# Two small transposes moved from TensorE to VectorE, in blocks of 32, in a fused window-attention and expert kernel

## The chip, the core and the metric

The kernel runs on one core of a Trainium2 chip. The core has a matmul engine (TensorE, PE in the profile), a vector engine (VectorE, DVE), a scalar engine (ScalarE, ACT), GpSimd (POOL), and SyncE (SP), whose queue issues most of the transfers here. They run side by side and wait for each other by semaphores. The metric is device time in microseconds; 4548.22 us is the median of three runs of the kernel before (4543.13 to 4551.57).

## The reference, cut to what matters

The input x is (2, 128, 256, 256) in float32: 131,072 pixels ("tokens") of 128 channels. One layer adds two things to it.

```
x = x + conv(ln_c(x))        # window attention, 8x8 windows, keys from 12x12, 4 heads of 32
t = tokens(x)
t = t + ffn(ln_t(t))         # 8 experts, the best two of each token

def ffn(x):
    p = softmax(x @ router_w + router_b)
    top_p, top_i = top_k(p, 2);  top_p = top_p / sum(top_p)
    y = einsum('bnd,edc->bnec', x, expert_w) + expert_b
    return sum over the two of top_p * y[top_i]
```

`ln_c` and `ln_t` normalise each token over its 128 channels. The mask of the attention leaves only keys whose row and column offsets have the right parity, so queries split into four interleaved "planes".

The change touches how, for each token, the mean, the mean square and the router's eight raw logits become gates (eight weights, of which two aren't zero) and two scale or shift values, and how these reach the places where they are used.

## The kernel before

**Tiling.** The image is cut into strips of eight rows; a strip has four planes of 512 queries. One turn of the main loop (`for n in range(n_planes + 7)`) handles one plane's attention, prepares the next plane's projections, and runs one expert "row" of 512 tokens (two image rows) of the strip before. There are 256 planes, and some turns at the end without attention. Channels lie on the 128 partitions. Tokens lie along the free dimension, 512 to a row, in NT = 4 groups of 128.

**Order.** The loop stands under a manual schedule: instructions stand on each engine in the order in which the code calls them. Functions are generators; each `next(...)` emits one piece of one. Each engine works its own queue in order. At the start of a turn PE's instructions are aligned (`addr_align(BLOCK, ...)`, L786).

**The row's statistics and gates.** `norms` (L531) squares the source (L541, ScalarE) and multiplies source and square by the narrow matrix `rw` (L547, PE). This puts, for each group t of 128 tokens, the logits (8), mean and mean square into the 32 partitions 32t to 32t+31 of the PSUM tile `plt`, with tokens along the columns. ScalarE copies it to SBUF (`lT`, L555) and PE transposes it whole into `plg` (L558), so that tokens lie on partitions: 128 partitions x (4 groups x 32 values). `rstd` (L227 to L234, with two exponents on ScalarE, L231 and L232) gives the reciprocal deviation. `norms` can serve two rows at once: f, the row for the experts, and c, a row for the attention's own normalisation.

`route` (L582 to L615, VectorE) makes logits, ranks, and gates, into `g`: 128 partitions x 40 columns, of which 32 are gates (expert by group), 4 the shift (`sd`, L590) and 4 the scale of row c (L567).

`spread` (L622 to L630) transposes g on PE into `pg`, copies it by ScalarE into `gT` (L624), writes gT to a DRAM tile `gd` (L626), and reads row c's scale back, broadcast to all partitions, as `rb` (L630). The experts read their gates back in the same way: `fetch` reads one expert's 512 gates into all 128 partitions (`gb`, L654), `fetch_means` the shift (`sb`, L659). All these reads stand in SyncE's queue.

**The experts.** VectorE multiplies six of the eight (`xe` <- `xs`, `gb`, L670) and GpSimd two, after `behind(6)` (L674) has held GpSimd until VectorE's sixth is done. PE multiplies with the expert's weights and adds up in `acc` (L679); VectorE adds acc to x (L685).

**PSUM.** `mm_tile` hands out tiles from a ring of three (tag mm). A plane takes nine: pvv, pu, pk, pq, pg, plt, pvv, plg, po. A new tile waits until the one three before it has been read.

**Where things stand in a turn.** The part that the change moves is `spread`; it stands after all of the next plane's projections to pq:

```
next(ahead, None)                 # pvv
nxt.fetch(7, nc.scalar)
next(ahead, None)                 # pu, and its block transpose uT on VectorE (L385)
states[n + 1]["shift"]()          # uT -> auT -> au: the position bias's rows (L348, L353)
next(ahead, None); next(ahead, None)   # pk; pq
if gated: gd, rb1 = spread(...)   # pg
for e in (4, 6, 7, 5): ex.product(e)
```

The functions that the diff touches, with the profile's line numbers:

Of the kernel before, what the change touches and what calls it, by code (L numbers as in the profile page):

```python
# [1 line left out]

# [8 lines left out]
F32 = mybir.dt.float32  # L11
AF = mybir.ActivationFunctionType
ALU = mybir.AluOpType
# [3 lines left out]
P = 128  # L17
HEADS, DH = 4, 32
E = 8
# [31 lines left out]
def kernel(  # L51
# [16 lines left out]
    nc = tc.nc  # L68
# [450 lines left out]
    def out_project(n, state):  # L519
# [8 lines left out]
        nc.vector.tensor_add(xv, po.rearrange("p (m a s) -> p m a s", a=PR, s=4), xv)  # L528
        yield

    def norms(f, c, nm):  # L531

        g = small.tile([P, (E + 2) * NT], F32, tag="g", name=f"g{nm}")
        srcs = []
        for j, src in ((0, f and rows_of(*f)), (2, c and ln1_src(*c))):
            if src is None:
                continue
            sq = work.tile([P, CH], F32, tag=f"sq{j}", name=f"sq{j}{nm}", bufs=1)  # L540
            nc.scalar.activation(sq, src, AF.Square)  # L541
            srcs += [(j, src), (j + 1, sq)]
        yield
        plt = mm_tile(f"plt{nm}")
        for j, src in srcs:
            for t in range(NT):
                nc.tensor.matmul(  # L547
                    plt[32 * t : 32 * t + 32, :P],
                    lhsT=rw[:, j],
                    rhs=src[:, t * P : (t + 1) * P],  # L550
                    start=(j == srcs[0][0]),
                    stop=(j == srcs[-1][0]),
                )
        lT = work.tile([P, P], F32, tag="lT", name=f"lT{nm}")
        nc.scalar.copy(lT, plt[:, :P])  # L555
        yield
        plg = mm_tile(f"plg{nm}")
        nc.tensor.transpose(plg[:, :P], lT, ident)  # L558
        p4 = plg[:, :P].rearrange("p (t e) -> p t e", e=32)
        k0, k1 = (0 if f else 1), (2 if c else 1)  # L560
        r, u = rstd(p4, k0, k1, nm)
        rs = None
        if f:
            rs = small.tile([P, NT], F32, tag="rs", name=f"rs{nm}")
            nc.vector.scalar_tensor_tensor(rs, u[:, 0], 3.0, r[:, 0], ALU.add, ALU.mult)
        if c:
            nc.vector.scalar_tensor_tensor(  # L567
                g[:, (E + 1) * NT :], u[:, 1 - k0], 3.0, r[:, 1 - k0], ALU.add, ALU.mult
            )
        yield g, rs, p4  # L570

# [3 lines left out]
    def route(i, k, g, rs, p4):  # L575


        nm = f"{i}_{k}"
        rs = rs.unsqueeze(2)
        lg = small.tile([P, NT, E], F32, tag="lg", name=f"lg{nm}")  # L580
        by_e = [P, NT, E]
        nc.vector.tensor_tensor(lg, p4[:, :, 0:E], rs.broadcast_to(by_e), ALU.mult)  # L582
        nc.vector.tensor_tensor(lg, lg, rb.unsqueeze(1).broadcast_to(by_e), ALU.add)
        mx = small.tile([P, NT, 1], F32, tag="mx2", name=f"mx2{nm}")
        nc.vector.tensor_reduce(mx, lg, AX.X, ALU.max)
        nc.vector.tensor_tensor(lg, lg, mx.broadcast_to(by_e), ALU.subtract)
        nc.scalar.activation(lg, lg, AF.Exp)
        sd = small.tile([P, NT, 1], F32, tag="sd", name=f"sd{nm}")
        nc.vector.reciprocal(sd, rs)
        nc.vector.tensor_tensor(  # L590
            g[:, E * NT : (E + 1) * NT].unsqueeze(2), sd, p4[:, :, E : E + 1], ALU.subtract
        )
        yield

        cmp = small.tile([P, NT, E, E], F32, tag="cmp", name=f"cmp{nm}")
        nc.vector.tensor_tensor(
            cmp,
            lg.unsqueeze(2).broadcast_to([P, NT, E, E]),
            lg.unsqueeze(3).broadcast_to([P, NT, E, E]),
            ALU.subtract,  # L600
        )
        nc.vector.tensor_tensor(
            cmp, cmp, ties.unsqueeze(1).broadcast_to([P, NT, E, E]), ALU.is_ge
        )
        rank = small.tile([P, NT, E], F32, tag="rank", name=f"rank{nm}")
        nc.vector.tensor_reduce(rank, cmp, AX.X, ALU.add)
        yield
        gate = small.tile([P, NT, E], F32, tag="gate", name=f"gate{nm}")
        nc.vector.scalar_tensor_tensor(gate, rank, 1.5, lg, ALU.is_lt, ALU.mult)
        sm = small.tile([P, NT, 1], F32, tag="sm2", name=f"sm2{nm}")  # L610
        nc.vector.tensor_reduce(sm, gate, AX.X, ALU.add)
        nc.vector.reciprocal(sm, sm)
        nc.vector.tensor_tensor(sm, sm, rs, ALU.mult)
        g1 = g[:, 0 : NT * E].rearrange("p (e t) -> p t e", t=NT)
        nc.vector.tensor_tensor(g1, gate, sm.broadcast_to(by_e), ALU.mult)  # L615
        yield

    def spread(f, c, g, nm):

        lo, hi = (0 if f else (E + 1) * NT), ((E + 2) * NT if c else (E + 1) * NT)  # L620
        pg = mm_tile(f"pg{nm}")
        nc.tensor.transpose(pg[: hi - lo, :P], g[:, lo:hi], ident)  # L622
        gT = small.tile([(E + 2) * NT, P], F32, tag="gT", name=f"gT{nm}")
        nc.scalar.copy(gT[: hi - lo], pg[: hi - lo, :P])  # L624
        gd = dram.tile([(E + 2) * NT, P], F32, tag="gd", name=f"gd{nm}")
        nc.sync.dma_start(gd[lo:hi], gT[: hi - lo])  # L626
        rb = None
        if c:
            rb = gates.tile([P, NT * P], F32, tag="rb", name=f"rb{nm}", bufs=2)
            nc.sync.dma_start(rb, to_all(gd, E + 1))  # L630
        return gd, rb
# [139 lines left out]
    with tc.manual_schedule(engines={ET.PE, ET.DVE, ET.Activation, ET.Pool, ET.SP}):  # L771
        for n in range(n_planes + 7):
            i, pl = divmod(n, 4)
            score, attn, outp, ahead, norm, rout = none, none, none, none, none, none
            if n < n_planes:
                score = scores(n, states[n])
                attn = attend(n, states[n])
                outp = out_project(n, states[n])
            if n + 1 < n_planes:
                states[n + 1] = {}  # L780
                ahead = project(n + 1, states[n + 1])

            if 6 <= n < n_planes:
                nc.tensor.addr_align(BLOCK, offset=BLOCK - FIRST_LIMIT)  # L786


            next(score, None)
            new, row = NoExperts(), None  # L790
            if gated and gated[0]:
                rout = route(*gated[0], *gated[2])
            next(rout, None)
            nxt.fetch(5, nc.scalar)
            for _ in rout:
                pass
            next(score, None)
            next(ahead, None)
            nxt.fetch(7, nc.scalar)
            next(ahead, None)  # L800
            if n + 1 < n_planes:
                states[n + 1]["shift"]()
            next(ahead, None)
            next(ahead, None)
            if gated:
                f, c, made = gated
                gd, rb1 = spread(f, c, made[0], f"_{n}")
                row = (*c, rb1) if c else None
                new = Experts(*f, gd) if f else new
            for e in (4, 6, 7, 5):  # L810
                ex.product(e)


            f = (i - 1, pl) if 0 < i <= len(strips) else None
            c = row_at(n)
            if f or c:
                norm = norms(f, c, f"_{n}")
            next(norm, None)
            next(attn, None)
            nxt.means()  # L820
            new.fetch_means()
            for e in (0, 1, 2, 3):
                nxt.times(e, dve)
            new.fetch(0, dve)
            for e in (4, 6):
                nxt.times(e, dve)
            new.fetch(1, dve)
            ex.end()
            new.fetch(2, dve)
            next(attn, None)  # L830
            next(attn, None)


            ex = nxt
            next(norm, None)
            load_x((n + 9) // 4, (n + 9) % 4, paced=True)
            new.fetch(3, dve)
            while to_store:
                store(*to_store.pop())
            next(ahead, None)  # L840
            ex.product(0)
            made = next(norm, None)
            ex.product(1)
            ex.product(2)
            new.fetch(4, nc.scalar)
            nxt.behind(6)
            nxt.times(5, pool)
            if row:
                ln1(*row, pool)
            if pl == 3 and i + 2 < len(strips):  # L850
                halo(i + 2)
            nxt.times(7, pool)
            if n + 2 < n_planes:
                columns(n + 2)
            next(outp, None)
            ex.product(3)
            next(outp, None)
            new.fetch(6, dve)
            gated, nxt = (f, c, made) if made else None, new
            states.pop(n, None)  # L860
# [58 lines left out]
```

The softmax here doesn't subtract the row's maximum and nothing guards it: scores larger than these inputs give would overflow.

## Time and profile before

| what | value |
|---|---|
| time, median of three | 4548.22 us |
| profiled execution | 4547.9 us, mean granted TensorE clock 0.997 |
| the transpose plg, PE (L558) | 260 times, mean 273 ns |
| the copy lT, ScalarE (L555) | 260 times, mean 266 ns |
| the transpose pg, PE (L622) | 245 times with 40 columns of g, mean 270 ns |
| the copy gT, ScalarE (L624) | 245 times with 40 rows, mean 259 ns |
| the write gd (L626) | 245 times with 20.0 KB |
| block transposes of 128x512 on VectorE | L385 and L505 717 ns (from PSUM), L510 711 ns (from SBUF) |
| bytes moved | 824.84 MB, 181 GB/s, 457,786 packets |

How to read it: a row of the groups gives line, engine, operation, tiles (out<-in), shape, count, busy time and mean duration, and then the idle time of the engine just before these instructions and who ended it. Matmuls are pipelined, so their durations overlap; what one takes out of PE's stream is read from the chain of work, where each piece is listed from its predecessor's end. In a timeline, a line gives start, length, engine, line and operation; a bracket gives how long the engine stood idle before it and who released it.

### The profile page before, as it was taken

Reading aid. Unit: us, or ns where it says so; the run is one execution under the profiler, and the core shown is the slowest. Engines: PE = TensorE matmul, PEld = TensorE weight load, DVE = VectorE, ACT = ScalarE, POOL = GpSimd, SP = SyncE. Lnnn points to the kernel's source line nnn. Section 1 sums busy time; section 2 is a strip of 40 time slices with the busy share of each in tenths; the row PEclk is TensorE's granted clock in tenths of the full one; section 3 lists DMA queues with packets and bytes.
Section 4 is the critical chain, followed back from the end, with each engine's and each line's share of the span. In section 5 each row is a group of like instructions: output and inputs, shape, how many; then the busy total and the mean of one; then the engine's idle time right before and its main releaser. Section 6 shows DMA issues by size and latency. Waiting matters only on the chain.

```text
span 4547.9 us, 224166 instructions
## 1 busy us (share of the span) xinstructions
PE 4490.6 (99%) x96841; PEld 2708.2 (60%) x96841; DVE 3826.1 (84%) x11330; ACT 1582.6 (35%) x4542; POOL 1321.7 (29%) x1812
## 2 busy tenths in 40 slices
PE   7999999999999999999999999999999999999997
PEld 5665666565666666666666666666666656656653
DVE  5888888888888888888888888888888888888886
ACT  3333333333333333333333333333333333333331
POOL 1232323232323223232323232323232323232221
PEclk9999999999999999999999999999999999999999
DMA  2565666566556666665656665656666656666655
GB/s 76 176 191 180 190 179 191 181 190 180 189 180 189 183 186 184 186 185 183 188 181 186 183 188 181 190 180 190 180 190 180 191 179 190 182 187 181 188 163 181
DMA packets 457786, 824.84 MB, mean 181 GB/s; under 512 B 52480, under 2 KB 64356, under 8 KB 456804
## 3 DMA queue, kind: packets, MB, share of 16 engines
q1 hardware_dynamic: 456074, 810.21, 59.0%
q8 instruction: 769, 12.60, 1.1%
q14 instruction: 213, 1.74, 0.1%
q10 hardware_dynamic: 730, 0.29, 0.0%
HBM read 737.95 MB, written 72.34 MB: 178 GB/s over the span
## 4 chain that ended last, share of the span: by engine, by line
PE 97%; DVE 1%; issue 1%; DMA 0%; ACT 0%; POOL 0%; SPq 0%; ACTq 0%; DVEq 0%; POOLq 0%
PE acc L679 38%; PE pvv L368 12%; PE att L464 7%; PE att L495 6%; PE plt L547 6%; PE pu L383 5%; PE po L523 5%; PE pk L395 5%; PE pq L417 5%; PE att L447 3%; PE att L485 3%; PE pg L622 1%; PE plg L558 1%; DMA gb<-gd 0%; DVE xe L670 0%
## 5 line engine op out<-in xcount | busy, mean ns | idle before, releaser
L679 PE MATMUL acc<-xe,ew 128*128 128x512 f32 x4096 | 1921.7, 595 | 6.5 <-DVE xt L685 2.6
L679 PEld LDWEIGHTS acc<-xe,ew 128*128 128x128 f32 x4096 | 720.8, 191 | 788.1 <-issue 780.3
L670 DVE TENSOR_TENSOR xe<-xs,gb 128x512 f32<-128x512 f32 x1536 | 950.5, 686 | 10.9 <-DMA gb<-gd 2.2
L674 POOL COPY last<-xe 128x1 f32<-128x1 f32 x256 | 48.3, 189 | 3110.8 <-DVE gb L653 3103.7
L670 POOL TENSOR_TENSOR xe<-xs,gb 128x512 f32<-128x512 f32 x512 | 652.3, 1275 | 5.7 <-PE att L495 2.7
L368 PE MATMUL pvv<-wt,xcol 128*128 128x128 f32 x4096 | 595.1, 288 | 4.2 <-POOL xcol L330 3.1
L368 PEld LDWEIGHTS pvv<-wt,xcol 128*128 128x128 f32 x4096 | 497.2, 191 | 66.6 <-issue 51.9
L555 ACT COPY lT<-plt 128x128 f32<-128x128 f32 x260 | 69.3, 266 | 1141.3 <-PE plt L547 1141.3
L271 POOL TENSOR_TENSOR xn<-xt,rb 128x512 f32<-128x512 f32 x249 | 375.9, 1510 | 79.9 <-DMA rb<-gd 68.1
L464 PE MATMUL att<-qs,kcol 32*64 32x32 f32 x32768 | 391.7, 226 | 2.4 <-issue 2.4
L464 PEld LDWEIGHTS att<-qs,kcol 32*64 32x64 f32 x32768 | 390.3, 130 | 2.6 <-issue 2.6
L375 ACT COPY vv<-pvv 128x512 f32<-128x512 f32 x512 | 300.3, 586 | 207.4 <-PE pvv L368 191.4
L495 PEld LDWEIGHTS att<-pT,vv 64*32 64x32 f32 x32768 | 347.8, 105 | 36.7
L472 ACT ACTIVATE pT<-att 128x1024 f32<-128x1024 f32 x256 | 262.1, 1024 | 253.7 <-PE att L464 250.3
L495 PE MATMUL att<-pT,vv 64*32 64x32 f32 x32768 | 342.5, 200 | 0.0
L385 DVE STREAM_TRANSPOSE uT<-pu 128x512 f32<-128x512 f32 x256 | 183.5, 717 | 150.2 <-PE pu L383 150.2
L541 ACT ACTIVATE sq<-xt 128x512 f32<-128x512 f32 x505 | 292.1, 628 | 0.0
L353 DVE STREAM_TRANSPOSE au<-auT 128x512 f32<-128x512 f32 x256 | 269.2, 1051 | 9.0
L406 ACT COPY kcol<-pk 128x560 f32<-128x560 f32 (+2 forms) x344 | 174.3, 507 | 268.5 <-PE pk L395 265.7
L523 PE MATMUL po<-o,wt 128*128 128x512 f32 x512 | 261.8, 593 | 4.1 <-DVE r__0_619 L227 1.0
L383 PE MATMUL pu<-xn,wrel 128*128 128x512 f32 x512 | 263.6, 596 | 0.0
L417 PE MATMUL pq<-xn,wt 128*128 128x512 f32 x512 | 262.2, 593 | 0.5 <-issue 0.2
(2700 smaller groups left out, 5579.8 us busy)
## 6 DMA issues: line engine op xcount, KB each, us to landing
gb<-gd SPq DMA_DIRECT2D x2048, 256.0 KB
xt<-in_x_dram SPq DMA_DIRECT2D x256, 256.0 KB
sb<-gd SPq DMA_DIRECT2D x256, 256.0 KB
out_dram<-xt SPq DMA_DIRECT2D x256, 256.0 KB
rb<-gd SPq DMA_DIRECT2D x249, 256.0 KB
gd<-gT SPq DMA_DIRECT2D x245, 20.0 KB
ew<-in_L_ffn_expert_w_dram SPq DMA_DIRECT2D x1, 512.0 KB
eb<-in_L_ffn_expert_b_dram SPq DMA_DIRECT2D x1, 512.0 KB
```

The costliest lines, as they stand in the source:

```text
L271: eng.tensor_tensor(xn[i % 2][:, :, :, k, 1 : PC + 1], ln1_src(i, k).rearrange("p (y j x) -> p y x j", y=2, x=2), rb.rearrange("p (y j x) ...
L368: nc.tensor.matmul(pv[:, t * P : (t + 1) * P], lhsT=xl[:, t0 + t].rearrange("p a k -> p (a k)"), rhs=wv, start=True, stop=True,)
L375: nc.scalar.copy(vv[:, t0 : t0 + 4, :].rearrange("p t c -> p (t c)"), pv)
L383: nc.tensor.matmul(pu, lhsT=wrel, rhs=inner, start=True, stop=True)
L417: nc.tensor.matmul(pq, lhsT=wq, rhs=inner, start=True, stop=True)
L464: nc.tensor.matmul(sc[rows, h, 32 * t : 32 * t + 32], lhsT=kk[hp, half * HP + t, :], rhs=qs[hp, m0 : m0 + 2].rearrange("p m a s -> p (m a ...
L495: nc.tensor.matmul(av[hp, half, 32 * t : 32 * t + 32], lhsT=vv[rows, t, hp], rhs=pT[rows, h, 32 * t : 32 * t + 32], start=True, stop=True,)
L523: nc.tensor.matmul(po, lhsT=wo, rhs=state["o"].rearrange("p f z -> p (f z)"), start=True, stop=True)
L541: nc.scalar.activation(sq, src, AF.Square)
L547: nc.tensor.matmul(plt[32 * t : 32 * t + 32, :P], lhsT=rw[:, j], rhs=src[:, t * P : (t + 1) * P], start=(j == srcs[0][0]), stop=(j == srcs ...
L670: eng.tensor_tensor(self.xe[e], self.xs, self.gb.pop(e), ALU.mult)
L679: nc.tensor.matmul(self.acc, lhsT=ew[:, e, :], rhs=self.xe.pop(e), start=(e == 0), stop=not self.xe)
```

## The change

Both full transposes and both copies go. `norms` transposes `plt` on VectorE in 32x32 blocks straight into `plg`, also in PSUM. As tokens were on columns in four blocks of 32, the result has token i of block b of group t on partition 32t+i and its values in columns 32b onward, and no longer one group to 32 columns. Arithmetic on g and plg doesn't mind. `g` becomes a fixed tile of 2 blocks of 32 columns (32 gates; and sd, row c's scale and zeros), three of them in turn, cleared once at the start by GpSimd. `spread` turns its blocks on VectorE into `gT`, and two writes of 32 columns each put them into `gd`, which now has 64 rows: first the half with shift and scale, then the gates. The address pattern of the write brings tokens back into order, in runs of 32 values (128 bytes). And `spread` moves up: it stands after the first piece of the next projection (pvv) and `fetch(7)`, ahead of pu and the position bias's rows. PE thus loses two instructions a plane, the PSUM ring one tile of nine.

```diff
+    gboth = [ctile([P, 2, NT, E], f"g{i}") for i in range(3)]
+    g_turn = itertools.count()
+    for g in gboth:
+        nc.gpsimd.memset(g, 0.0)
...
-        g = small.tile([P, (E + 2) * NT], F32, tag="g", name=f"g{nm}")
+        g = gboth[next(g_turn) % len(gboth)]
...
-        lT = work.tile([P, P], F32, tag="lT", name=f"lT{nm}")
-        nc.scalar.copy(lT, plt[:, :P])
         yield
         plg = mm_tile(f"plg{nm}")
-        nc.tensor.transpose(plg[:, :P], lT, ident)
+        nc.vector.transpose(plg[:, :P], plt[:, :P])
...
-                g[:, (E + 1) * NT :], u[:, 1 - k0], 3.0, r[:, 1 - k0], ALU.add, ALU.mult
+                g[:, 1, :, 1], u[:, 1 - k0], 3.0, r[:, 1 - k0], ALU.add, ALU.mult
...
-            g[:, E * NT : (E + 1) * NT].unsqueeze(2), sd, p4[:, :, E : E + 1], ALU.subtract
+            g[:, 1, :, 0:1], sd, p4[:, :, E : E + 1], ALU.subtract
...
-        g1 = g[:, 0 : NT * E].rearrange("p (e t) -> p t e", t=NT)
-        nc.vector.tensor_tensor(g1, gate, sm.broadcast_to(by_e), ALU.mult)
+        nc.vector.tensor_tensor(g[:, 0], gate, sm.broadcast_to(by_e), ALU.mult)
...
     def spread(f, c, g, nm):
-        lo, hi = (0 if f else (E + 1) * NT), ((E + 2) * NT if c else (E + 1) * NT)
-        pg = mm_tile(f"pg{nm}")
-        nc.tensor.transpose(pg[: hi - lo, :P], g[:, lo:hi], ident)
-        gT = small.tile([(E + 2) * NT, P], F32, tag="gT", name=f"gT{nm}")
-        nc.scalar.copy(gT[: hi - lo], pg[: hi - lo, :P])
-        gd = dram.tile([(E + 2) * NT, P], F32, tag="gd", name=f"gd{nm}")
-        nc.sync.dma_start(gd[lo:hi], gT[: hi - lo])
+        gT = small.tile([P, 2, 32], F32, tag="gT", name=f"gT{nm}")
+        nc.vector.transpose(
+            gT.rearrange("p k i -> p (k i)"), g.rearrange("p k b j -> p (k b j)")
+        )
+        gd = dram.tile([2 * E * NT, P], F32, tag="gd", name=f"gd{nm}")
+        to = gd.rearrange("(k j t) (b i) -> k (t b) j i", k=2, j=E, i=32)
+        for k in (1, 0):
+            if k or f:
+                nc.sync.dma_start(to[k], gT[:, k])
...
             nxt.fetch(7, nc.scalar)
+            if gated:
+                f, c, made = gated
+                gd, rb1 = spread(f, c, made[0], f"_{n}")
+                row = (*c, rb1) if c else None
+                new = Experts(*f, gd) if f else new
             next(ahead, None)
...
             next(ahead, None)
             next(ahead, None)
-            if gated:
-                f, c, made = gated
-                gd, rb1 = spread(f, c, made[0], f"_{n}")
-                row = (*c, rb1) if c else None
-                new = Experts(*f, gd) if f else new
             for e in (4, 6, 7, 5):
                 ex.product(e)
```

More of the change, by code (lines that the diff above doesn't have):

```diff
@@ L1 @@
+import itertools
 from contextlib import ExitStack
```

## The prediction

> **What bounds the kernel now.** I read the busy shares first, then the chain of work that ended last, then that chain over one plane, then the other engines over the same plane.
>
> ```profile
> PE 4490.6 (99%) x96841; PEld 2708.2 (60%) x96841; DVE 3826.1 (84%) x11330; ACT 1582.6 (35%) x4542; POOL 1321.7 (29%) x1812
> ...
> PE 97%; DVE 1%; issue 1%; DMA 0%; ACT 0%; POOL 0%; SPq 0%; ACTq 0%; DVEq 0%; POOLq 0%
> ```
>
> PE holds 97% of the chain, so a microsecond taken out of PE's stream in the loop should come off the end, and work on another engine costs nothing until it makes PE wait. The chain over one plane shows what the two transposes to be removed take there (start, length, piece):
>
> ```profile
> 2000.43 0.86 PE pq L417 x2
> 2001.29 0.11 PE pg L622
> 2001.40 3.44 PE acc L679 x8
> ...
> 2008.66 0.86 PE acc L679 x2
> 2009.52 0.11 PE plg L558
> 2009.63 1.72 PE acc L679 x4
> ```
>
> pg begins the moment pq ends and acc begins 0.11 us later; the same at plg. The mean of 270 ns in the table of groups is latency, not what PE gives up: its stream advances by 0.11. The plane's period is 2023.95 - 2006.56 = 17.39 us (the same piece, plt, one plane later in a longer answer of this view). Now VectorE over the same plane, since it takes over the work:
>
> ```profile
> 2009.10 0.06 DVE L653 MEMSET gb<- 128x1 f32 x1
> 2009.67 0.17 DVE L227 COPY r__114_37583<-plg 128x8 f32<-128x8 f32 x1 [0.51 <-PE plg L558]
> 2009.87 0.50 DVE L228 TENSOR_TENSOR u__114_37582<-r__114_37583 128x8 f32<-128x8 f32 x1
> ...
> 2011.89 0.16 DVE L567 SCALAR_TENSOR_TENSOR g<-u__114_37582,r__114_37583 128x4 f32<-128x4 f32 x1
> 2012.24 0.69 DVE L528 TENSOR_TENSOR xt<-po,xt 128x512 f32<-128x512 f32 x1 [0.20 <-PE po L523]
> ...
> 2016.24 0.22 DVE L615 TENSOR_TENSOR g<-gate,sm 128x32 f32<-128x32 f32 x1
> 2017.00 0.72 DVE L385 STREAM_TRANSPOSE uT<-pu 128x512 f32<-128x512 f32 x1 [0.54 <-PE pu L383]
> ```
>
> VectorE waits for PE three times a plane: 0.51 for plg, 0.20 for po, 0.54 for pu. So it is not the bound, but only about 1.25 us a plane from being it. GpSimd's line in the same window explains L228:
>
> ```profile
> 2009.08 1.27 POOL L670 TENSOR_TENSOR xe<-xs,gb 128x512 f32<-128x512 f32 x1
> ```
>
> L228 multiplies a tile of 8 columns by itself and lasts 0.50 instead of the 0.17 of its neighbours. It ends at 2010.37, GpSimd's product at 2010.35.
>
> **What the Trainium skill says.** "SBUF — State Buffer", section "Who interferes with whom": a VectorE instruction with two SBUF inputs and a GpSimd instruction that reads SBUF exclude each other, and whichever issues second waits for the first to finish; one with at most one SBUF input doesn't contend outside the two-port modes. The trace agrees: L228 (two SBUF inputs) ends with GpSimd's product, L227 (input in PSUM) runs beside it at 0.17. So the statistics can't get past L228 before GpSimd's xe(7) is done, however early they start, and the new transpose of plt (one input, in PSUM) may run beside GpSimd. "VectorE: DVE Perf Modes", section "The three transpose paths": VectorE turns independent 32x32 blocks only. That is why the layout of g and of the writes changes. "DMA: Bandwidth & Descriptors", section "Specifications": below 512 B a transfer loses line rate to a read-modify-write. The new writes go in runs of 128 B; no run here shows that yet, so I bound it.
>
> **The change part by part.**
>
> PE loses plg and pg: 2 x 0.11. From the products, where a pass of 512 columns takes 0.43, a pass of 128 is 0.1075; I take 0.215 a plane. New period 17.39 - 0.215 = 17.175, if nothing else takes over. Over the 250 or so planes in which PE is the bound: 54 us.
>
> ScalarE loses the copies lT (266 ns x 260) and gT (259 ns x 245). It is at 35%; worth nothing by itself.
>
> VectorE gains two block transposes. Their price: 128x512 transposes take 717 ns from PSUM (L385) and 711 ns from SBUF (L510). A slope comes from elementwise rows: 192 ns at 32 columns (L583), 425 at 256 (L596), 686 at 512 (L670), so 1.04 ns a column. Estimates: plt to plg, 128 columns, 717 - 384 x 1.04 = 318 ns; g to gT, 64 columns, 711 - 448 x 1.04 = 245 ns. No row shows one that writes PSUM or is this short: the lower ends are the 185 ns or so that any small instruction on VectorE takes, the upper ends the 512-column durations. I take 0.32 and 0.25.
>
> Where they land. The plt transpose: VectorE is free at 2009.16, plt has been complete since 2007.57, so it runs 2009.16 to 2009.5 in place of the 0.51 wait for plg. Then L227 ends at 2009.65 and L228 waits for GpSimd until 2010.37 as it does today. Up to 1.0 us this transpose costs nothing. The g transpose comes after L615 and before L385, inside the 0.54 wait for pu.
>
> Does VectorE still make it in 17.175? I count one turn from the start of L385 (1999.61 in this plane): xe(6) ends at +6.4, which releases GpSimd (its "last" copy at 2006.17 waits for just that); GpSimd's xe(7) and with it L228 end at +10.76; the exponents on ScalarE and L567 bring it to +12.44; L528 to L615 take 4.22 without the wait for po: +16.66. With the new transpose: +16.91. So in most planes 0.26 us remains. Every fourth plane has a halo copy on GpSimd (621 ns, L245) ahead of xe(7): 17.53 there, 0.36 over. Averaged, 16.91 + 0.155 = 17.07, still under 17.175. The 0.36 lag is absorbed: PE's needs from VectorE come late, o ends at 2009.15 and po loads at 2010.76 (1.6 us), xt at 2006.65 and acc's next product at 2008.50 (1.8 us).
>
> New waits on PE. The PSUM ring of three (tag mm) now sees 8 tiles a plane and not 9, so users change neighbours: plt waits for uT to have left pu, pvv for the plt transpose, po for pvv's copy by ScalarE. In time: uT leaves at 2000.33 against plt at 2006.49; the plt transpose ends at about 2009.5 against pvv at 2014.94; vv's copy ends at 2009.29 against po's load at 2010.76, 0.1 of which goes. All are met with over a microsecond; nothing is queued behind them.
>
> Gates. Today gT is written at 2002.09 and the queue waits about 1.2 us for it ahead of rb:
>
> ```profile
> SPq L630 <- DMA gd<-gT: 302.6, 249, 2.5
> ```
>
> In the new order the first write can issue at about 2016.8 - 17.39 = 1999.4 on this scale, 2.7 us earlier, but behind gb(7) of the same queue, and there are two writes of 16 KB, 128 runs of 128 B each, in place of one of 20 KB in 40 rows. rb waits for the first only. Bounds for each landing: today's 1.2 us below; above, 1.2 plus 1.4 (256 KB of gb at the 181 GB/s of the page) with the run part doubled, some 4 us. gb(0) isn't asked for before 2004.87, so even 4 us is hidden; the bias row gets to GpSimd (2007.61) no later than now. The padding adds 65,000 small packets to 458,000, and q1 stands at 59% of 16 engines: no queue fills.
>
> The ends. In the last planes PE has no scores and stands still for this:
>
> ```profile
> PE pg L622 <- DVE g L615: 17.5, 6, 3.5
> ```
>
> pg stood ahead of acc's last four products, so they waited for the gates of the next rows; without it they don't. VectorE then sets the pace of these five planes: it also waited 1.31 for plg (ahead of 4476.09) and now waits only for plt. I estimate 1 us off each of five: 5 us. The start: nothing.
>
> Sum: 54 + 5 = 59 us; 4548 - 59 = 4489.
>
> **The rivals.**
>
> *VectorE with GpSimd becomes the bound.* For it: the spare 0.1 us on average, and a transpose price that no row shows. Its turn is 16.82 + the price of the g transpose; it meets 17.175 at 0.36 us. At 0.50: 17.32, 250 x 0.07 saved, 4530; at the upper 0.72: 17.54, 4586, a loss. Against it: the first transpose is hidden up to 1.0 us, and both known transposes follow one slope with other VectorE work. 12%; its likely part lies at 4505 to 4530.
>
> *Gates come late, PE slower than before.* If short runs hold each write over 5 us, sb and gb(0) to gb(2) slip in the in-order queue, then VectorE's xe and GpSimd's ln1. Half a microsecond a plane gives 4548 - 54 + 128 = 4622. Against it: 2.7 us of head start and 5 us until the first gb. 5%.
>
> *No gain in the stream.* PE's blocks of instructions are aligned once a plane, and four fewer instructions mean about as many more no-ops. If each removed 0.11 only turns into padding or a load gap: 4546. Against it: before L447, behind today's padding, PE's stream shows no gap (acc ends and L447 starts at 2013.07). 3%.
>
> **How the numbers follow.** Forecast 80%, VectorE 12%, gates 5%, no gain 3%. Predicted 4489. Low 4476: 0.11 exactly twice on 260 planes (57) and a tail that gains three times as much. High 4509: the milder half of the VectorE rival. Faster by over 0.2% (under 4539): 0.80 and nearly all of the 12%, 0.91. Within: 0.04. Slower: 0.05.
>
> **What would show it.** Right: a period of 17.17; no plg or pg on the chain; VectorE's wait for plg gone and L228 lengthened to 0.7; the wait for pu near 0.3; gd's first write ahead of L385's end. Wrong: PE waits of over 0.1 a plane named after VectorE at po or acc (the VectorE rival), after DMA or rb (the gates), or a gap ahead of L447 (padding). The step most likely to be off is the price of the g transpose.

## The result, and the profile after

| | before | after |
|---|---|---|
| median | 4546.16 us (4543.13 to 4551.57, 4 runs) | 4484.72 us (4481.92 to 4490.74, 4 runs) |
| ratio | | 0.9865, 95% interval 0.9848 to 0.9882 |
| profiled execution | 4547.9 us | 4480.1 us |

The kernel is faster by 1.35%, some 61 us; the two profiled executions differ by 67.8. The first part of the page after, busy time and share of the span of each engine, and the row of the groups for the transpose ahead of which VectorE still waits for PE:

```profile
PE 4422.6 (99%) x96321; PEld 2683.3 (60%) x96321; DVE 3996.2 (89%) x11850; ACT 1467.7 (33%) x4022; POOL 1317.7 (29%) x1815
...
L386 DVE STREAM_TRANSPOSE uT<-pu 128x512 f32<-128x512 f32 x256 | 182.8, 714 | 78.0 <-PE pu L384 77.0
```

PE's busy time fell by 68.0 us, as much as the span, so PE still sets the end. (The chain of work in the page after breaks off near its end, so what follows goes by timelines.) Its 520 fewer instructions are 260 plt transposes and 260 gate transposes. VectorE's busy time rose by 170 us, from 84% to 89%, and it still waits for PE ahead of uT: it isn't the bound.

PE over one plane, in its timeline (start, length, then the operation; lengths overlap). The first line is the plt of this plane, the sixth that of the next:

```profile
1995.05 0.43 PE L554 MATMUL plt<-xt,rw 128*32 128x128 f32 x8
...
2004.39 1.02 PE L384 MATMUL pu<-xn,wrel 128*128 128x512 f32 x2
2005.25 1.02 PE L396 MATMUL pk<-xn,wt 128*128 128x512 f32 x2
2006.11 1.02 PE L418 MATMUL pq<-xn,wt 128*128 128x512 f32 x2
2006.97 3.59 PE L686 MATMUL acc<-xe,ew 128*128 128x512 f32 x8
...
2012.22 0.43 PE L554 MATMUL plt<-xt,rw 128*32 128x128 f32 x8
...
2013.23 1.16 PE L369 MATMUL pvv<-wt,xcol 128*128 128x128 f32 x8
2014.22 2.74 PE L686 MATMUL acc<-xe,ew 128*128 128x512 f32 x6
2016.80 1.02 PE L524 MATMUL po<-o,wt 128*128 128x512 f32 x2
```

acc follows pq with no pg between, and the six passes after pvv (three products of two passes each) are one piece where plg split them. The period is 2012.22 - 1995.05 = 17.17 us. VectorE and GpSimd in the same plane:

```profile
2005.01 0.19 DVE L619 TENSOR_TENSOR g<-gate,sm 128x32 f32<-128x32 f32 x1
2005.23 0.24 DVE L625 STREAM_TRANSPOSE gT<-g 128x64 f32<-128x64 f32 x1
2005.45 0.72 DVE L386 STREAM_TRANSPOSE uT<-pu 128x512 f32<-128x512 f32 x1
...
2014.21 0.69 DVE L516 TENSOR_TENSOR o<-att,rT 128x512 f32<-128x512 f32 x1
2014.83 0.33 DVE L563 STREAM_TRANSPOSE plg<-plt 128x128 f32<-128x128 f32 x1
...
2015.19 0.17 DVE L228 COPY r__116_37780<-plg 128x8 f32<-128x8 f32 x1
2015.39 0.83 DVE L229 TENSOR_TENSOR u__116_37779<-r__116_37780 128x8 f32<-128x8 f32 x1
```
```profile
2014.93 1.27 POOL L677 TENSOR_TENSOR xe<-xs,gb 128x512 f32<-128x512 f32 x1
```

The g transpose fills the old wait for pu, and the plt transpose the old wait for plg. L229 (L228 of before) now lasts 0.83: it ends at 2016.22, GpSimd's product at 2016.20. So what stands behind it is still timed by GpSimd's product, and not by the transpose ahead of it. The transposes' prices, in the groups:

```profile
L563 DVE STREAM_TRANSPOSE plg<-plt 128x128 f32<-128x128 f32 x260 | 84.8, 326 | 0.2 <-PE plt L554 0.2
...
L625 DVE STREAM_TRANSPOSE gT<-g 128x64 f32<-128x64 f32 x260 | 63.7, 245 | 8.7
```

Where the 67.8 us of the pair lie, by the starts of the scores in PE's trace:

| stretch | before | after | saved |
|---|---|---|---|
| start to plane 10's scores | 183.36 | 181.94 | 1.4 |
| plane 10's to plane 245's scores | 4097.7 | 4035.1 | 62.6 |
| plane 245's scores to the end | 266.9 | 263.1 | 3.8 |

The middle is the whole matter, and it holds more than the removed passes. The next table takes PE's stream apart in planes 10 to 244, without 13 planes around the boundary of the two images. "Stretched" counts planes in which a piece took over 0.025 us longer than its median, with the sum of what it took longer:

| | before | after |
|---|---|---|
| shortest plane | 17.384 us | 17.163 us |
| median plane | 17.408 | 17.165 |
| mean plane | 17.432 | 17.168 |
| pg stretched | 21 planes, 2.9 us | (gone) |
| acc stretched | 33 planes, 3.0 us | 6 planes, 0.8 us |
| last attention products (L495, after L496) stretched, up to plt | 74 planes, 3.8 us | none |

The shortest plane lost 0.221 us, twice 0.11. Times 235 planes that is 52 us of the 62.6. Of the other 11 us, the stretched pieces of this table make 8.9 (9.7 before, 0.8 after): small stalls of PE that the kernel before had and this one, but for six planes, hasn't. The experiments look into both.

### The profile page after: what moved, and what is told of

It is laid out like the page before. It is cut to its first block, busy times and chain, and to the rows that moved or that the text cites. A ratio compares the mean times of both kernels' runs of the same rounds, so it can differ in the third digit from the quotient of the medians.

```text
span 4480.1 us, 224632 instructions
## 1 busy us (share of the span) xinstructions
PE 4422.6 (99%) x96321; PEld 2683.3 (60%) x96321; DVE 3996.2 (89%) x11850; ACT 1467.7 (33%) x4022; POOL 1317.7 (29%) x1815
## 5 line engine op out<-in xcount | busy, mean ns | idle before, releaser
L686 PE MATMUL acc<-xe,ew 128*128 128x512 f32 x4096 | 1889.0, 594 | 19.6 <-DVE gb L660 18.8
L686 PEld LDWEIGHTS acc<-xe,ew 128*128 128x128 f32 x4096 | 758.8, 190 | 885.7 <-issue 861.8
L272 POOL TENSOR_TENSOR xn<-xt,rb 128x512 f32<-128x512 f32 x249 | 375.0, 1506 | 66.5 <-DMA rb<-gd 55.9
L496 PEld LDWEIGHTS att<-pT,vv 64*32 64x32 f32 x32768 | 348.0, 105 | 39.4 <-issue 2.5
L496 PE MATMUL att<-pT,vv 64*32 64x32 f32 x32768 | 343.2, 200 | 2.3 <-issue 2.3
L396 PE MATMUL pk<-xn,wt 128*128 128x512 f32 (+2 forms) x528 | 261.0, 578 | 0.0
```

The lines of the kernel that those rows point to most:

```text
L272: eng.tensor_tensor(xn[i % 2][:, :, :, k, 1 : PC + 1], ln1_src(i, k).rearrange("p (y j x) -> p y x j", y=2, x=2), rb.rearrange("p (y j x) ...
L496: nc.tensor.matmul(av[hp, half, 32 * t : 32 * t + 32], lhsT=vv[rows, t, hp], rhs=pT[rows, h, 32 * t : 32 * t + 32], start=True, stop=True,)
L686: nc.tensor.matmul(self.acc, lhsT=ew[:, e, :], rhs=self.xe.pop(e), start=(e == 0), stop=not self.xe)
```

## The experiments

Ratios are to the kernel before, measured beside each run. Plane figures are those of the table above, on each run's own trace.

**Each half alone: e1_stats_only and e2_gates_only.** The kernel after, with the gates' part put back to what it was before (e1), or with the statistics' part put back (e2):

```diff
 e1: in spread, at its old place behind pq
-        nc.vector.transpose(gT..., g...)          # and two writes of 32 columns
+        pg = mm_tile(f"pg{nm}")
+        nc.tensor.transpose(pg[: hi - lo, :P], g[:, lo:hi], ident)
+        nc.scalar.copy(gT[: hi - lo], pg[: hi - lo, :P])
+        nc.sync.dma_start(gd[lo:hi], gT[: hi - lo])
 e2: in norms
-        nc.vector.transpose(plg[:, :P], plt[:, :P])
+        nc.scalar.copy(lT, plt[:, :P])
+        nc.tensor.transpose(plg[:, :P], lT, ident)
```

> One half of the change alone: plt is block-transposed by VectorE, while the gates are still transposed by PE, copied by ScalarE and written once, at their old place behind pq. The order of the tokens is not restored in the write, so gates reach other tokens of their row; the work is the same. Theory (two causes: 0.11 us of PE's stream for each transpose, and small stalls that hang on the gates' transpose and on the ring of nine tiles): the shortest plane is 17.385 - 0.11 = 17.275 us, the stalls behind pg and ahead of plt stay (in total some 0.04 us a plane), so 4546 - 28 = 4518. Rival (the 0.267 us a plane that came off are halved evenly between the transposes): 0.133 a plane, 4513, and no stalls behind pg. The times lie close; the stalls in the trace tell.

> The other half alone: the gates are block-transposed by VectorE at the early place with two writes, while plt is still copied by ScalarE and transposed whole by PE. The order of the tokens is not restored in the write, so gates reach other tokens; the work is the same. Theory (stalls hang on pg and on the ring of nine): shortest plane 17.275 us, next to no stalls, so 250 x (0.11 + 0.045) = 39 off, 4507. Rival (even halves): 4513, stalls still there in half of the planes.

| | e1_stats_only | e2_gates_only |
|---|---|---|
| time | 4528.68 us (4527.81 to 4530.98) | 4512.00 us (4510.18 to 4515.07) |
| ratio | 0.9954 (0.9938 to 0.9971) | 0.9917 (0.9902 to 0.9931) |
| shortest plane, mean plane | 17.275, 17.328 | 17.275, 17.280 |
| pg stretched | 19 planes, 3.8 us | (no pg) |
| acc stretched | 39 planes, 3.5 us | 7 planes, 0.8 us |
| last attention products stretched | 57 planes, 3.0 us | none |

The kernel before, measured beside them, took 4551.39, so the halves gained 22.7 and 39.4 us. The product of the ratios, 0.9954 x 0.9917 = 0.9871, agrees with the 0.9865 of both together: the halves add up. Each takes 0.109 off the shortest plane, one pass. What else there is belongs to the gates' half alone: with it the stretched planes go, without it all three kinds stay. e1 fell 5 us short of the 28 expected. Its shortest plane is as expected and its remaining stalls are as large as those of before; between the scores of planes 10 and 245 its trace gains 25.1 us. What is missing lies at the start: plane 10's scores begin at 187.3 us and not at 183.4, and 1.8 of these 3.9 us are a longer gap at the first alignment (5.72 us against 3.91, see e7).

**The place of the gates: e3_late.** The kernel after, with `spread` at its old place, behind pq:

```diff
             nxt.fetch(7, nc.scalar)
-            if gated:
-                gd, rb1 = spread(f, c, made[0], f"_{n}")
 ...
             next(ahead, None)
             next(ahead, None)
+            if gated:
+                gd, rb1 = spread(f, c, made[0], f"_{n}")
             for e in (4, 6, 7, 5):
```

> The changed kernel with spread back at its old place, behind pq; both transposes stay on VectorE. Theory (the early place is needed, since two writes land 3.0 us after issue and rb 3.3 after that): gT is ready at about 2007.8 on the changed kernel's scale, the first write lands at about 2010.9, rb at about 2014.3, while GpSimd now takes it at 2013.5; GpSimd's row, xe(7) and VectorE's statistics slip by 0.8 us a plane, VectorE's turn becomes 17.6 to 17.7 us, total 4590 to 4620, with GpSimd waiting for rb in most planes. Rival (the place is worth nothing, since the gates are used a plane later and the transpose fits elsewhere in VectorE's order): 4485, within 8.

It took 4495.26 us (4492.71 to 4505.05), ratio 0.9883 (0.9868 to 0.9898). My theory failed in its size. The late writes and the new wait are there. From the waits of e3 between 200 and 4200 us (total, count, longest), and its transfers (KB each, median us from issue to landing):

```profile
POOL xn L272 <- DMA rb<-gd: 72.5, 140, 1.4
...
gd<-gT SPq DMA_DIRECT2D x516, 16.0 KB, 2.6
```

GpSimd stands waiting for rb, the scale of row c, in 140 planes, 0.52 each, where the kernel after has no such wait in that stretch. But most of this doesn't reach PE: the mean plane is 17.194 against 17.168 (acc is stretched in 24 planes, 5.9 us), some 6 us in all. The medians of e3 and of the kernel after lie 8 us (by the ratios) to 10.5 us apart, and their intervals overlap, so the times alone don't tell the early place from nothing; the planes of the traces put it at some 6 us. In the kernel after, the same writes take longer to land but issue early:

```profile
gd<-gT SPq DMA_DIRECT2D x516, 16.0 KB, 3.0
rb<-gd SPq DMA_DIRECT2D x249, 256.0 KB, 3.3
```
```profile
2005.70 1.16 SPq L633 DMA_DIRECT2D gd<-gT  x2
2008.73 0.33 SPq L637 DMA_DIRECT2D rb<-gd  x1
```

In the timeline above, rb is asked for at 2008.73, and GpSimd's product that reads it (L272) begins at 2013.47, 4.7 us later.

**How far VectorE's first transpose is hidden: d1_plt_three.** The transpose of plt three times over:

```diff
         nc.vector.transpose(plg[:, :P], plt[:, :P])
+        nc.vector.transpose(plg[:, :P], plt[:, :P])
+        nc.vector.transpose(plg[:, :P], plt[:, :P])
```

> The changed kernel in which VectorE turns plt into plg three times in a row (the result is the same): 2 x (0.326 + about 0.03) = 0.71 us more of VectorE a plane. Theory (what follows, L229, waits for GpSimd's product anyway: its mean is 0.82 us in three of four planes and 1.24 in the fourth, against 0.17 without that wait, so 0.65 to 1.07 is covered): the extra work disappears in that wait, L229 shrinks to about 0.17 in most planes, the time stays within 0.2% of the changed kernel, ratio to the kernel before 0.985 to 0.989. Rival (VectorE's total work is what counts, and its mean spare time is 0.21 us a plane): 0.5 us a plane more, ratio 1.01 to 1.02.

It took 4488.44 us (4486.58 to 4489.90), ratio 0.9870 (0.9855 to 0.9885): no difference from the kernel after that the runs can tell, with the mean plane at 17.173. The three last 326 + 332 + 332 = 990 ns, so this lies at the edge of the 1.0 us that the prediction counted as free. In three planes of four L229 shrank in the mean to 0.37 to 0.41 us from 0.81 to 0.84, and the wait for pu from 0.27 to 0.12. So the wait for GpSimd didn't take all of it: over 60 planes, of the 0.73 us that two more transposes add from start to start, L229 gave up 0.50, and the waits for po and pu some 0.21.

**How near VectorE is to being the bound: d2_gates_three.** The transpose of g three times over (two more calls like the one shown):

```diff
         nc.vector.transpose(
             gT.rearrange("p k i -> p (k i)"), g.rearrange("p k b j -> p (k b j)")
         )
+        nc.vector.transpose(gT..., g...)
+        nc.vector.transpose(gT..., g...)
```

> The changed kernel in which VectorE turns g into gT three times in a row (the result is the same): 2 x (0.245 + about 0.03) = 0.55 us more of VectorE a plane, at the place whose spare time, the wait for pu, is 0.27 us in three of four planes and 0.01 in the fourth. Theory (GpSimd and VectorE form one turn that is 0.2 us shorter than PE's): VectorE becomes the bound by 0.55 - 0.21 = 0.34 us a plane, 80 us more than the changed kernel, ratio to the kernel before 1.001 to 1.008, and PE starts to wait for VectorE. Rival (PE alone is the bound, VectorE has 11% to spare, which is 1.9 us a plane): no change, ratio 0.985 to 0.989.

It took 4521.88 us (4521.74 to 4527.70), ratio 0.9947 (0.9932 to 0.9962): 37 us more than the kernel after, where the two theories had 80 and almost nothing. One plane of its VectorE:

```profile
1020.82 0.19 DVE L619 TENSOR_TENSOR g<-gate,sm 128x32 f32<-128x32 f32 x1
1021.05 0.25 DVE L625 STREAM_TRANSPOSE gT<-g 128x64 f32<-128x64 f32 x1
1021.33 0.24 DVE L628 STREAM_TRANSPOSE gT<-g 128x64 f32<-128x64 f32 x1
1021.61 0.25 DVE L631 STREAM_TRANSPOSE gT<-g 128x64 f32<-128x64 f32 x1
1021.77 0.67 DVE L386 STREAM_TRANSPOSE uT<-pu 128x512 f32<-128x512 f32 x1
```

No wait for pu is left. PE's planes are stretched now between the end of pvv and the first product of acc (61 planes, 17.8 us, 53 of them the planes after a halo copy of GpSimd) and within acc (115 planes, 11.2 us); the mean plane is 17.297. One of the 61:

```profile
785.19 1.16 PE L369 MATMUL pvv<-wt,xcol 128*128 128x128 f32 x8
786.64 2.84 PE L692 MATMUL acc<-xe,ew 128*128 128x512 f32 x6 [0.29 <-DVE gb L666]
785.90 0.68 DVE L698 TENSOR_TENSOR xt<-acc,xt 128x512 f32<-128x512 f32 x1
```

The new acc begins 0.06 us after VectorE has read the old one (L698 ends at 786.58): PE waits for VectorE (the bracket names the short memset that VectorE ran just then). So VectorE with GpSimd does become the bound, as the theory says, and above all in every fourth plane, where the prediction saw nothing to spare. The size failed, and VectorE's starts over 90 planes show by what. From the start of the first gT transpose to the start of uT it is 0.73 us where the kernel after has 0.44: 0.28 more, where my 80 us came from 0.34. But 0.10 of that comes back ahead of L529, where VectorE no longer stands waiting for po, and 0.04 between uT and the next start. This leaves 0.14 a plane, beside the 0.13 by which the mean plane grew.

**The stalls at a boundary of 256 instructions: e4_limit_99.** `addr_align` puts a fixed place of the plane at a fixed place in blocks of BLOCK = 256 PE instructions. Before, a boundary fell exactly between pg and the first pass of acc (351 = 95 + 256 instructions into the plane, as I counted them). After, two instructions fewer stand ahead of it, pg's weight load and its pass, and it falls behind the first pass of acc. In e1, which keeps pg, it falls where it fell before, and the stalls are there; in e2, which has no pg, they are gone but for 7 planes. A stretched plane of the kernel before:

```profile
431.76 1.02 PE L417 MATMUL pq<-xn,wt 128*128 128x512 f32 x2
432.62 0.27 PE L622 MATMUL pg<-ident,g 128*40 128x128 f32 x1
433.00 1.55 PE L679 MATMUL acc<-xe,ew 128*128 128x512 f32 x3
```

acc starts 0.38 after pg and not 0.11. If the place of the boundary does this, moving it by four instructions in the kernel before should end it:

```diff
-BLOCK, FIRST_LIMIT = 256, 95
+BLOCK, FIRST_LIMIT = 256, 99
```

> The kernel before with one constant changed (FIRST_LIMIT 95 to 99): the places where PE's instructions cross from one aligned block of 256 to the next move by four instructions, so the crossing that lay exactly between pg and acc's first pass now lies behind acc's second pass. Theory (the stalls behind pg are waits for the next block of instructions, seen because only a 0.11 us pass covers them): the 20 planes with a stretched pg and the 30 with a stretched acc fall to a handful, 6 us less, 4540. Rival (they come from transfers or from other engines): as many such planes as before, 4546.

It took 4544.15 us (4540.45 to 4546.56, 20 runs), ratio 0.9984 (0.9977 to 0.9991): 7.2 us faster. The same plane:

```profile
432.15 1.02 PE L417 MATMUL pq<-xn,wt 128*128 128x512 f32 x2
433.01 0.27 PE L622 MATMUL pg<-ident,g 128*40 128x128 f32 x1
433.12 2.31 PE L679 MATMUL acc<-xe,ew 128*128 128x512 f32 x5
```

Not one plane is stretched at pg or acc any more (21 and 33 before); at the last attention products 71 still are, 3.5 us. So the position of the boundary makes the pg and acc stalls, and 5 us (by the pieces of the table) to 7 us (by e4's times) of the change's gain came from having moved it, by accident. That it is the next block's arrival that PE waits for is inferred from this; no view names it.

**The stalls ahead of plt: f1_ring_of_nine.** These stay in e4 and e1 and are gone in e2 and after. With nine tiles a plane in a ring of three, plt takes the place of a tile that ScalarE has read, and the trace of before has a semaphore wait of 51 ns on PE ahead of plt, behind 128 short products with their 128 weight loads: 255 such waits in all. With eight tiles plt takes the place of pu, which VectorE has read, and 8 such waits are left. To bring the ninth tile back without its transpose, an empty tile stands where pg stood:

```diff
             next(ahead, None)
+            pad = mm_tile(f"pad{n}")
+            nc.vector.memset(pad[:, 0:1], 0.0)
             for e in (4, 6, 7, 5):
```

> The changed kernel with a ninth, empty tile taken from the PSUM ring at pg's old place; VectorE clears one column of it (59 ns), PE does nothing. So plt again follows pk in its slot and waits for two engines, which costs PE an extra wait instruction ahead of plt. Theory (the stretched ends of the attention's products ahead of plt in 76 planes of the kernel before are that instruction, which the sequencer has to run right behind 256 short ones): they come back in 55 to 80 planes, 3 to 4 us in total, the shortest plane stays 17.165. Rival (they came from other traffic): at most five such planes.

It took 4492.73 us (4490.59 to 4496.72), ratio 0.9881 (0.9866 to 0.9895). The waits are back, 251 of them, and so are the stalls, in 70 planes, 3.5 us (before: 74 and 3.8), with the shortest plane unchanged at 17.164. So the ring's ninth tile makes them, and the gates' half removed them. The memset itself, 59 ns on VectorE, came along and may have its part in the rest: the median plane is 0.013 longer too, 3 us over 235 planes.

**The padding: e7_align_from_2.** The alignment fills the plane with instructions that do nothing, as many as the plane is short of whole blocks. The first alignment shows as a gap ahead of the scores, and it grew, from 3.91 us before (74 such instructions in the trace) to 6.75 after (104) (a bracket gives the gap and who ended it; "issue" means that no wait shows):

```profile
113.13 1.16 PE L448 MATMUL att<-au,keys 32*64 32x128 f32 x32 [6.75 <-issue]
```
```profile
113.68 1.16 PE L447 MATMUL att<-au,keys 32*64 32x128 f32 x32 [3.91 <-issue]
```

I tried to bring the alignment forward, to planes in which PE waits anyway:

```diff
-            if 6 <= n < n_planes:
+            if 2 <= n < n_planes:
```

> The changed kernel with PE's alignment from the third plane on instead of the seventh. Theory (the first alignment fills up to 255 places with no-ops that PE has to run, 6.75 us ahead of L448 in the changed kernel against 3.91 before; in the first planes PE waits for other engines anyway): the gap goes and with it 3 to 7 us, ratio to the kernel before 0.984 to 0.986. Rival (the first planes' pace is set by PE's instructions as well, so the gap only moves): same as the changed kernel.

It took 4501.52 us (4500.35 to 4501.95), ratio 0.9898 (0.9882 to 0.9915), some 15 us slower than the kernel after. Theory and rival were both wrong. The early planes are shorter in instructions, and each pays for its own padding, with 118, 73, 77 and 46 instructions that do nothing:

```profile
65.56 1.16 PE L448 MATMUL att<-au,keys 32*64 32x128 f32 x32 [7.72 <-issue]
83.30 1.16 PE L448 MATMUL att<-au,keys 32*64 32x128 f32 x32 [4.29 <-issue]
100.79 1.16 PE L448 MATMUL att<-au,keys 32*64 32x128 f32 x32 [4.61 <-issue]
115.85 1.16 PE L448 MATMUL att<-au,keys 32*64 32x128 f32 x32 [2.31 <-issue]
```

## Why the prediction held, step by step

**PE's share: right.** 0.215 a plane was the estimate, 0.221 the measurement, 0.109 from each half alone. The row of the groups says 270 ns for such a transpose; the chain's 0.11 was the one to use.

**The stream's sum: too small.** 54 us was forecast, 62.6 came in the middle stretch alone. The term that was missing is PE's small stalls: 5 to 7 us at the block boundary (e4) and nearly 4 ahead of plt (f1). The change removed both without aiming at either. The prediction had looked at one plane, in which none shows; a mean over all planes (17.437) beside the shortest (17.384) would have shown 0.05 a plane, 12 us, that isn't in any row.

**The prices: right.** 0.318 and 0.245 by the slope; 326 and 245 ns measured, and PSUM as target costs nothing to speak of. The Trainium skill, "VectorE: DVE Perf Modes", section "The three transpose paths", gives 311 ns for 128x128 in bf16 by this path and 390 ns for TensorE's; the 326 here are float32 and agree in size, but the comparison that counted was with 0.11 of PE's stream, not with 390.

**The first transpose hidden: right, and shown.** The wait for plg went, L229 lengthened (to 0.81 to 0.84 in most planes; I had said 0.7), and d1 filled the counted 1.0 us without loss of time, though 0.2 us of it came out of later waits of VectorE. What the Trainium skill's "SBUF — State Buffer", section "Who interferes with whom" says of one and two SBUF inputs fits both ways: L563, with its input in PSUM, kept its 0.33 beside GpSimd, and L229, with two inputs in SBUF, ended with GpSimd's product.

**VectorE's turn: right in place and size.** Mean wait for pu by plane, in the order of planes 0 to 3 of a strip:

| | plane 0 | 1 | 2 | 3 |
|---|---|---|---|---|
| before | 0.536 us | 0.474 | 0.535 | 0.529 |
| after | 0.275 | 0.012 | 0.265 | 0.277 |
| forecast | 0.26 | none | 0.26 | 0.26 |

The halo plane has nothing to spare and its lag is absorbed, as forecast. The rival "VectorE becomes the bound" didn't happen, but d2 shows that it was near: two more transposes of 245 ns a plane brought it about, and cost 37 us.

**The ring's new waits: right** that none costs anything; missed that an old one, ahead of plt, went.

**The gates: hidden, as forecast,** landing in 3.0 us where the bounds were 1.2 and 4. The first write issues 0.47 us ahead of uT's end. That the early place is what hides it was too strong: with the late place e3 loses some 6 us by its planes. On the Trainium skill's "DMA: Bandwidth & Descriptors", section "Specifications" (line rate lost below 512 B): the 16 KB writes in runs of 128 B took 2.6 us to land even when issued late, and how much of that the runs' size makes was not separated.

**The ends: partly mis-sized.** In the rows without attention VectorE's wait for PE went, as forecast. The lines are the first statistics instruction of the first and the last of four such rows, before and after:

```profile
4476.09 0.16 DVE L227 COPY r__256_83804<-plg 128x4 f32<-128x4 f32 x1 [1.31 <-PE plg L558]
...
4515.28 0.16 DVE L227 COPY r__259_84140<-plg 128x4 f32<-128x4 f32 x1 [1.31 <-PE plg L558]
```
```profile
4411.29 0.16 DVE L228 COPY r__256_82779<-plg 128x4 f32<-128x4 f32 x1
...
4447.63 0.16 DVE L228 COPY r__259_83103<-plg 128x4 f32<-128x4 f32 x1
```

Three turns take 39.19 and 36.34 us, 0.95 a row, against 1 forecast. But the whole end gained only 3.8, and ten planes of attention in it should have brought 2.2 of their own. Padding took it back: in the last six planes with scores a gap of 0.28 to 0.50, 2.5 us in all, stands ahead of L448. These planes have fewer instructions (no row c) and so more padding: the trace has 46 instructions that do nothing in each, where the kernel before has 41 there and no gap. In the planes of the middle there are 14 against 9, and no gap in either. The five more are the two passes, their two weight loads and the wait ahead of plt. That was the rival "padding" (which had counted four), seen in these six planes and at the first two alignments, and nowhere else. Of PE's long wait at the end only the name changed: pg for g (17.5 us) became acc for gb (18.8), both VectorE's.

The terms that were off, stalls up by nearly 11 us and the ends down by some 4, leave 67.8 in the profiled pair and 61 between the medians against 59 forecast. That the total came so near is partly luck: two errors of opposite sign, and a profiled pair that lies further apart than the medians. What stays open is the cause inside PE of the two stalls, and the exact value of the early place.

## What to carry to other kernels

Price an instruction on the bounding engine by what the stream advances, not by its duration, and on the engine that takes it over by the wait that it fills; then repeat the moved piece two and three times to learn how much of that wait is left. Before forecasting from one plane, set the shortest period beside the mean of all: the difference is time that rows and waits don't show, and an edit that shifts instructions or buffers can remove it or bring it. When a removed tile changes which engine frees the next one's buffer, look for waits that go as well as for waits that come.

## What the runs showed of the hardware that was not expected

- A boundary of a block of 256 PE instructions behind a pass of 0.11 us stalled PE in 21 of 222 planes (0.03 to 0.56 us) and the products after it in 33 (mostly 0.10); four instructions further on it stalled none (e4).
- A ninth tile in the ring, which puts a semaphore wait ahead of plt behind some 256 short instructions, cost about 0.05 us in a third of the planes, though the semaphore that it waits for had last been raised some 1.5 us earlier (before, e4, f1).
- The padding of the alignment hides up to a point: in the last planes 41 instructions that do nothing show no gap ahead of the scores (before), 46 show 0.28 to 0.50 us (after), and a first alignment, with 74 to 118, shows 3.9 to 7.7 us.
- A block transpose of float32 on VectorE writes PSUM at its usual price (326 ns for 128 columns, three in a row 326, 332, 332), beside a GpSimd product or not.
